# Linear attention by chunks of 128 tokens, its energies and its running state taken by halves of 64

## The chip, the cores and the metric

One Trainium2 chip, one core. The metric is the device time of one execution in microseconds (us): the median of three timed runs of the kernel before is 874.49 us (873.55 to 876.25). The profile shown below is of one further execution.

## The reference, cut to what matters

The layer is an attention block without softmax (B = 16 sequences, N = 512 tokens, D = 128, 16 heads of 8), two layer norms, and a feed-forward part with a shared expert and 8 routed ones (two per token). Only the attention is touched by the change:

```python
q = silu(x @ Wq);  k = silu(x @ Wk);  v = x @ Wv       # 16 heads of 8
q = concat([q * cos(ang), q * sin(ang)])               # 16 features a head, k likewise
energy = einsum('bhnd,bhmd->bhnm', q, k) * tril(ones)
out = einsum('bhnm,bhmd->bhnd', energy, v) @ Wo
out = layernorm(out * sigmoid(x @ G1 @ G2)) * gamma + beta
x = layernorm(x + out)
...
x = layernorm(x + shared_expert(x) + routed_experts(x))
```

There is no softmax, so what all tokens of the past give to a query can be summed up in a state: for each head the 16 x 8 matrix sum of k v. A query takes its own neighbourhood by energies and everything earlier by the state.

## The kernel before, in words

**Stages.** From 0 to about 377 us runs the attention: 64 chunks t of 128 tokens, four to a sequence (c = t mod 4). To about 500 us follow the rest of the routing and of its scatters beside the shared expert, then the routed experts, the rest of the shared expert and the sums at the end. All matrix work is in 32-bit floats, which TensorE does in two passes: a product written once appears twice in the profile.

**The loop** (L791) is software-pipelined. Round t issues, in this order on every engine: `project(t+2)`, one step of the shared expert (`shared`), `turn_over(t+1)`, another step, one step of `after(b)` (output projection, norms, logits of a finished sequence), `energies(t)`, `values(t-1)`, `remember(t+1)`, scatters, more steps of `after` and of the routing. The shared expert feeds from round 14 on: an "up" step is a product of 512 columns with a silu on ACT (L138) or a multiplication on DVE (L150), a "down" step four products of 128 columns (L159). Rounds come in runs of one kind or the other. Engines work their lists in order.

**A chunk.**

- `project`: two products give q, k, the gate and v (L415, L418) into one PSUM tile `pq`; ACT takes out q with a silu (L422), k with a silu (L423), the gate (L426), v into the padded tile `vpad` (L430, 128 partitions) and, one half of the partitions at a time, into `vlow` (L436, twice). DVE multiplies by cosines and sines (L440, tile `hat`). For every second head the k and v rows are turned: the late 64 tokens lie in partitions 0 to 63.
- `turn_over`: four transposes (L453) into `pt`; ACT copies kT (L455), q with one or the other head of each pair set to zero (L459, L460), a copy of a part of that (L461, which waits for L460), and qT (L463).
- `energies`: 16 products (L498) on tiles of 32 rows by 64 columns of the array: four row groups (two heads each) and two halves of the keys, 192 columns each: 64 early queries and 64 late ones of one head, 64 late ones of the other. Each row group g writes a PSUM bank of its own. DVE multiplies each bank with the causal mask (L505, four of 128x384).
- `values`: into `pout`, on tiles of 128 rows by 32 columns (four column groups at once): 4 products of the state with qT, 128 columns (L522, not for c = 0), 8 with `vlow` (L531) and 16 with `vpad` (L540), 64 columns each. ACT copies it out (L546).
- `remember`: 8 products (L476), again 128 by 32, give k v of the whole chunk; DVE masks off the other heads (L483 for c = 0, L486), POOL adds the state so far (L487). For the last chunk of a sequence nothing is done.

**Buffers.** All PSUM tiles but the energies' come from one pool of four banks, `ps_w`: pq, pt, pout, pst and those of the shared expert and of `after`. A new tile takes the bank that was given free first, and its first product waits for that tile's last reader.

Of the kernel before, what the change touches and what calls it, by code (L numbers as in the profile page):

```python
# [10 lines left out]
F32 = mybir.dt.float32  # L11
I32 = mybir.dt.int32
AF = mybir.ActivationFunctionType
# [25 lines left out]
PI_BELOW = 3.141592  # L39

# [6 lines left out]
def tile_kernel(  # L47
# [146 lines left out]
    with ExitStack() as ph:  # L194
# [21 lines left out]
        with tc.manual_schedule(engines=ORDERED):  # L216
# [51 lines left out]

            NVP = 4
            vpads = []  # L270
            for i in range(NVP):
                vp = cst.tile([P, 4, 4, 40], F32, name=f"vpad{i}")

                vl = cst.tile([P, 8, 40], F32, name=f"vlow{i}")
                vpads.append((vp, vl))
                if i < 2:
                    nc.gpsimd.memset(vp, 0.0)
                    nc.gpsimd.memset(vl, 0.0)
# [11 lines left out]
            for vp, vl in vpads[2:]:  # L290
                nought(vp.rearrange("p a b d -> p (a b d)"), 640)
                nought(vl.rearrange("p a d -> p (a d)"), 320)
# [24 lines left out]

        def sines(c):

            for s, (from_, scale, bias) in enumerate([(scratch[:, NC + c], -1.0, half_pi), (scratch[:, c], 1.0, 0.0)]):  # L320
                for to, n0, n1 in ((cst_tok[:, c, 0], 0, D), (cst_tok[:, c, 1, 1::2], D, D + HALF)):
                    nc.scalar.activation(
                        to[:, :, s, :], from_[:, n0:n1].rearrange("p (h d) -> p h d", d=8), AF.Sin,
                        scale=scale, bias=bias,
                    )

        def same(c):

            nc.vector.tensor_copy(
                cst_tok[:, c, 1, 0::2].rearrange("p h s d -> p h (s d)"),  # L330
                cst_tok[:, c, 0, 0::2].rearrange("p h s d -> p h (s d)"),
            )

        with tc.manual_schedule(engines=ORDERED):
            angles(0, pth)
            sines(0)
            angles(1, th_sb)
            same(0)

            causal = cst.tile([P, 3, HALF], F32, name="causal")
            nc.gpsimd.tensor_tensor(causal[:, 0, 0:1], scratch[:, 0, 0:1], zcol, ALU.mult)
            nc.gpsimd.memset(causal, 1.0)
            bmask = cst.tile([P, 64], F32, name="bmask")
            nc.gpsimd.memset(bmask, 1.0)
            nc.gpsimd.affine_select(
                bmask, bmask, pattern=[[-16, 8], [0, 8]], compare_op=ALU.is_ge, fill=0.0, base=0, channel_multiplier=1
            )
            nc.gpsimd.affine_select(  # L350
                bmask, bmask, pattern=[[16, 8], [0, 8]], compare_op=ALU.is_ge, fill=0.0, base=15, channel_multiplier=-1
            )
            for block, at in ((0, 0), (0, HALF), (1, HALF), (2, 0)):
                rows = causal[at : at + HALF, block, :]
                nc.gpsimd.affine_select(
                    rows, rows, pattern=[[1, HALF]], compare_op=ALU.is_ge, fill=0.0, base=0, channel_multiplier=-1
                )
            expi = cst.tile([P, E], I32, name="expi")
            expf = cst.tile([P, E], F32, name="expf")
            first = cst.tile([P, E], F32, name="first")  # L360
            startrow = cst.tile([P, E], F32, name="startrow")
            goes_on = {}
            for n in sorted({(b1 - b0) * NC for b0, b1 in groups}):
                goes_on[n] = cst.tile([P, E, n + 1], F32, name=f"goes_on{n}")
            tri = cst.tile([P, P], F32, name="tri")
            toki = cst.tile([P, NT], I32, name="toki")
            sloti = cst.tile([P, NS], I32, name="sloti")
# [40 lines left out]
        hats, qkt, ets, states, gates, oTs = {}, {}, {}, {}, {}, {}  # L408


        def project(t):
# [11 lines left out]
            nc.scalar.activation(qk[:, D:].rearrange("p (h d) -> p h d", d=16), pq[:, 0:8, 16:32], AF.Silu)  # L423
            if c == 0:
# [4 lines left out]
            vp, vl = vpads[t % NVP]  # L429
            nc.scalar.copy(  # L430
                vp.rearrange("p a (c b) d -> p (a c) b d", b=2)[:, :, :, 0:8],
                pq[:, 8:16, 16:32].rearrange("p h (b d) -> p h b d", b=2),
            )
            for i in range(2):
                mine = slice(HALF * i, HALF * i + HALF)
                nc.scalar.copy(vl[mine, :, 8 * i : 8 * i + 8], pq[mine, 8:16, 16 + 8 * i : 24 + 8 * i])  # L436
# [10 lines left out]
        def turn_over(t):  # L447
# [9 lines left out]
            q2 = wk2.tile([P, 2, 6, HALF], F32, tag="q2", name=f"q2_{t}")  # L457
            halves = pt[:, 0].rearrange("p a (h n) -> p a h n", h=2)
            nc.scalar.activation(q2[:, :, 0:5:4, :], halves, AF.Copy, scale=par[:, 0:1])  # L459
            nc.scalar.activation(q2[:, :, 3:6:2, :], halves, AF.Copy, scale=par[:, 1:2])  # L460
            nc.scalar.copy(q2[:, :, 1:3, :], q2[:, :, 4:6, :])  # L461
# [4 lines left out]
        def remember(t):  # L466

            b, c = divmod(t, NC)
            hat = hats.pop(t)
            if c + 1 == NC:  # L470
                return
            vp = vpads[t % NVP][0]
            pst = ps_w.tile([P, 2, 64], F32, tag="w", name=f"pst_{t}")
            for s in range(2):
                for i in range(4):
                    nc.tensor.matmul(  # L476
                        pst[32 * i : 32 * i + 32, s, :], hat[:, 1, ds(s * P + 32 * i, 32)],
                        vp[:, 2 * s : 2 * s + 2, :, 0:8], start=True, stop=True,
                    )
            states[t] = new = wk3.tile([P, 2, 64], F32, tag="state", name=f"state_{t}")  # L480
            mask = bmask.unsqueeze(1).to_broadcast([P, 2, 64])
            if c == 0:
                nc.vector.tensor_tensor(new, pst, mask, ALU.mult)  # L483
            else:
                add = wk2.tile([P, 2, 64], F32, tag="add", name=f"add_{t}")
                nc.vector.tensor_tensor(add, pst, mask, ALU.mult)  # L486
                nc.gpsimd.tensor_tensor(new, states[t - 1], add, ALU.add)  # L487

        def energies(t):

            kT, q2, _ = qkt[t]
            pes = [ps_e.tile([P, 2, 3, HALF], F32, tag="e", name=f"pe_{t}_{g}") for g in range(4)]
            for s in range(2):
                for g in range(4):
                    rows = slice(32 * g, 32 * g + 32)
                    for i in range(2):
                        mine = slice(HALF * i, HALF * i + HALF)
                        nc.tensor.matmul(  # L498
                            pes[g][mine, s], kT[rows, s, mine], q2[rows, s, 3 * i : 3 * i + 3],
                            start=(s == 0), stop=(s == 1),  # L500
                        )
            ets[t] = []
            for g in range(4):
                et = etp.tile([P, 2, 3, HALF], F32, tag="et", name=f"et_{t}_{g}")
                nc.vector.tensor_tensor(  # L505
                    et.rearrange("p s k n -> p s (k n)"), pes[g].rearrange("p s k n -> p s (k n)"),
                    causal.rearrange("p k n -> p (k n)").unsqueeze(1).to_broadcast([P, 2, 3 * HALF]), ALU.mult,
                )
                ets[t].append(et)

        def values(t):

            b, c = divmod(t, NC)
            et, (vp, vl) = ets.pop(t), vpads[t % NVP]
            vp, vl = vp.rearrange("p a b d -> p (a b d)"), vl.rearrange("p a d -> p (a d)")
            _, _, qT = qkt.pop(t)
            pout = ps_w.tile([P, P], F32, tag="w", name=f"pout_{t}")
            if c > 0:
                state = states.pop(t - 1) if c == NC - 1 else states[t - 1]
                for a in (0, 2, 1, 3):  # L520
                    s = a // 2
                    nc.tensor.matmul(  # L522
                        pout[32 * a : 32 * a + 32, :], state[:, s, ts(a % 2, 32)], qT[:, s, :],
                        start=True, stop=False,
                    )

            for gg in range(2):
                for a in (0, 2, 1, 3):
                    s, g = a // 2, 2 * (a % 2) + gg
                    at = 40 * (4 * s + g) - 16 * gg  # L530
                    nc.tensor.matmul(  # L531
                        pout[32 * a : 32 * a + 32, 0:HALF], vl[:, at : at + 32], et[g][:, s, 0, :],
                        start=(c == 0 and gg == 0), stop=False,
                    )
            for gg in range(2):
                for j in range(2):
                    for a in (0, 2, 1, 3):
                        s, g = a // 2, 2 * (a % 2) + gg
                        at = a * 160 + 32 * (2 * gg + j)
                        nc.tensor.matmul(  # L540
                            pout[32 * a : 32 * a + 32, HALF:], vp[:, at : at + 32], et[g][:, s, 1 + j, :],
                            start=False, stop=(gg == 1 and j == 1),
# [247 lines left out]
        with tc.manual_schedule(engines=ORDERED):  # L790
# [47 lines left out]
            zero = vpads[0][0].rearrange("p a b d -> p (a b d)")[:, 0:N]  # L838
# [271 lines left out]
```

## Time and profile before

| what | value |
|---|---|
| the timed runs, median | 874.49 us (873.55 to 876.25) |
| the profiled execution | 865.53 us, its span 863.8 us |
| granted TensorE clock, mean | 0.988 |
| busy: PE, weight loads, DVE | 825.7, 568.8, 554.2 us |
| busy: ACT, POOL | 433.0, 337.2 us |
| energies, L498 | 2048 passes, 62.6 us busy |
| their masks, L505 | 256 instructions, 124.4 us, 547 ns each |
| values, L522, L531, L540 | 20.4, 26.6, 40.8 us busy |
| chunk's k v, L476 | 768 passes, 20.0 us busy |

Busy time is the time in which an engine had at least one instruction in flight. For PE the passes overlap, so the mean duration of one (340 ns in L498) is far longer than the step from one to the next. "PEld" is the loading of weights, which runs beside the products.

### The profile page before, as it was taken

What the parts mean: (1) busy time and instruction counts of PE and PEld (TensorE: products, weight loads), DVE (VectorE), ACT (ScalarE), POOL (GpSimd) and SP (SyncE); (2) the same over time, 40 slices, a digit from 0 to 9 for tenths busy, and PEclk for the clock granted to TensorE, in tenths of its full rate; (3) what the DMA queues carried; (4) which work ended last, traced back from release to release, by engine and by line L of the source; (5) the groups of instructions that cost most, each with busy time, mean ns of one, the idle gap of its engine ahead of it and who ended that gap; (6) DMA issues with size and microseconds to landing.
All of it is one profiled execution on the core that took longest, in us unless ns stands there. A gap on an engine that the chain in (4) does not pass through costs nothing. (4 is left out here: it accounts for less than half of the span.)

```text
span 863.8 us, 24377 instructions
## 1 busy us (share of the span) xinstructions
PE 825.7 (96%) x9776; PEld 568.8 (66%) x9776; DVE 554.2 (64%) x1629; ACT 433.0 (50%) x1279; POOL 337.2 (39%) x451
## 2 busy tenths in 40 slices
PE   6899999989999998899999998999999999999896
PEld 4666668756766865756666665777667776755664
DVE  7887888889988788975533335444434442387754
ACT  6876776675677677544222222333333333243345
POOL 2132122221666665587666641343333433211110
PEclk9999999999999999999999999999999999999999
DMA  6011111110111110048000032231122200365211
GB/s 199 21 34 33 34 33 33 34 33 15 51 56 56 59 46 21 21 163 295 22 10 6 0 99 79 94 95 53 63 90 93 62 28 25 92 178 169 78 37 49
DMA packets 66387, 57.45 MB, mean 67 GB/s; under 512 B 6180, under 2 KB 55132, under 8 KB 66274
## 3 DMA queue, kind: packets, MB, share of 16 engines
q1 hardware_dynamic: 59474, 44.95, 17.1%
q0 software_dynamic: 6656, 10.69, 3.8%
q8 instruction: 77, 1.26, 0.6%
q10 hardware_dynamic: 144, 0.26, 0.1%
q14 instruction: 36, 0.29, 0.1%
HBM read 32.62 MB, written 26.48 MB: 68 GB/s over the span
## 5 line engine op out<-in xcount | busy, mean ns | idle before, releaser
L725 POOL DMA_INDIRECT xg_dram<-x,idx x128 | 132.3, 1034 | 42.7 <-issue 40.9
L936 POOL DMA_INDIRECT y_dram<-y,to x80 | 77.6, 970 | 155.3 <-ACT y L934 155.3
L138 ACT ACTIVATE sl<-pg 128x512 f32<-128x512 f32 x128 | 75.6, 594 | 121.4 <-PE pg L136 114.7
L150 DVE TENSOR_TENSOR h<-sl,pu 128x512 f32<-128x512 f32 x128 | 87.6, 684 | 74.8 <-PE pu L149 57.7
L136 PE MATMUL pg<-x1T,sg_sb 128*128 128x512 f32 x256 | 132.2, 598 | 0.0
L149 PE MATMUL pu<-x1T,su_sb 128*128 128x512 f32 x256 | 130.9, 593 | 0.0
L159 PE MATMUL pd<-sd_sb,h 128*128 128x128 f32 x1024 | 125.1, 279 | 5.9 <-DVE x1T L164 5.7
L505 DVE TENSOR_TENSOR et<-pe,causal 128x384 f32<-128x384 f32 x256 | 124.4, 547 | 9.1 <-PE pe L498 8.7
L159 PEld LDWEIGHTS pd<-sd_sb,h 128*128 128x128 f32 x1024 | 121.3, 195 | 12.1 <-DVE x1T L164 6.3
L1024 DVE TENSOR_TENSOR eh<-esl,peu 128x512 f32<-128x512 f32 (+1 forms) x96 | 57.5, 599 | 109.8 <-PE peu L1021 107.2
L112 POOL TENSOR_TENSOR rstd<-ve,neghalf 128x4 f32<-128x4 f32 x46 | 49.5, 1076 | 195.1 <-DVE ve L110 188.8
L930 PEld LDWEIGHTS ped<-rd,eh 128*128 128x128 f32 x640 | 84.0, 192 | 24.1 <-issue 22.0
L1019 PE MATMUL peg<-xgT,rg 128*128 128x512 f32 (+1 forms) x192 | 84.6, 522 | 0.0
L1021 PE MATMUL peu<-xgT,ru 128*128 128x512 f32 (+1 forms) x192 | 84.4, 521 | 0.0
L930 PE MATMUL ped<-rd,eh 128*128 128x128 f32 x640 | 84.3, 275 | 0.0
L1023 ACT ACTIVATE esl<-peg 128x512 f32<-128x512 f32 (+1 forms) x96 | 50.5, 526 | 57.5 <-PE peg L1019 54.8
L149 PEld LDWEIGHTS pu<-x1T,su_sb 128*128 128x128 f32 x256 | 45.9, 191 | 44.9 <-issue 39.9
L934 ACT ACTIVATE y<-ped,wt 128x128 f32<-128x128 f32 x80 | 29.4, 367 | 85.7 <-PE ped L930 85.7
L136 PEld LDWEIGHTS pg<-x1T,sg_sb 128*128 128x128 f32 x256 | 44.7, 192 | 37.4 <-issue 34.1
L415 PE MATMUL pq<-W,xT 128*128 128x384 f32 x128 | 59.9, 551 | 7.5 <-DVE h L150 3.2
L498 PE MATMUL pe<-q,kT 32*64 32x192 f32 x2048 | 62.6, 340 | 0.8 <-DVE et L505 0.8
L1021 PEld LDWEIGHTS peu<-xgT,ru 128*128 128x128 f32 x192 | 36.5, 190 | 32.2 <-issue 28.9
(181 smaller groups left out, 1250.8 us busy)
## 6 DMA issues: line engine op xcount, KB each, us to landing
y_dram<-vpad SPq DMA_DIRECT2D x16, 512.0 KB, 7.3
y<-y_dram SPq DMA_DIRECT2D x32, 256.0 KB, 3.3
xT<-xt SPq DMA_DIRECT2D x15, 384.0 KB, 2.9
xg<-xg_dram SPq DMA_DIRECT2D x8, 660.0 KB, 4.5
x<-x SPq DMA_DIRECT2D x16, 256.0 KB, 3.5
o<-res SPq DMA_DIRECT2D x15, 256.0 KB, 2.8
xg_dram<-x,idx POOLq DMA_INDIRECT x128, 2.3
rg<-rg SPq DMA_DIRECT2D x8, 256.0 KB, 4.7
```

The lines of the kernel that those rows point to most:

```text
L136: nc.tensor.matmul(pg, sg_sb[:, ts(i, P)], seq, start=True, stop=True)
L138: nc.scalar.activation(sl, pg, AF.Silu)
L149: nc.tensor.matmul(pu, su_sb[:, ts(i, P)], seq, start=True, stop=True)
L150: nc.vector.tensor_tensor(h[i // half][:, i % half, :], h.pop(("s", i)), pu, ALU.mult)
L159: nc.tensor.matmul(pd, h[k][:, i - k * half, ts(c, P)], sd_sb[:, i, :], start=(i == 0), stop=(i == IS // P - 1))
L498: nc.tensor.matmul(pes[g][mine, s], kT[rows, s, mine], q2[rows, s, 3 * i : 3 * i + 3], start=(s == 0), stop=(s == 1),)
L505: nc.vector.tensor_tensor(et.rearrange("p s k n -> p s (k n)"), pes[g].rearrange("p s k n -> p s (k n)"), causal.rearrange("p k n -> p (k ...
L725: i = nc.gpsimd.indirect_dma_start(out=xg_dram[:, :], out_offset=bass.IndirectOffsetOnAxis(ap=idx[:, k, t : t + 1], axis=0), in_=x1[:, t, ...
L930: nc.tensor.matmul(pd, h[:, i, ts(c, P)], got[e][2][:, i, :], start=(i == 0), stop=(i == IR // P - 1))
L936: i = nc.gpsimd.indirect_dma_start(out=y_dram[:, :], out_offset=bass.IndirectOffsetOnAxis(ap=to[:, at : at + 1], axis=0), in_=y, in_offset ...
L1019: nc.tensor.matmul(pg[:, :n], rg_sb[:, ts(i, P)], xgTs[e][:, ds(o0, n)], start=True, stop=True)
L1021: nc.tensor.matmul(pu[:, :n], ru_sb[:, ts(i, P)], xgTs[e][:, ds(o0, n)], start=True, stop=True)
```

## The change

A chunk stays 128 tokens, but energies are taken only within its halves of 64 tokens; a state is kept at the middle of each chunk as well as at its end, and each half of the queries takes the state just before it. The turned heads are now two neighbours out of each four (they were every second one), so that the two heads of a row group lie alike.

- `project`: k in two silus (64 elements a partition each) to put the heads in the new order; v in four copies of 64 partitions into one tile `vpad` instead of one copy of 128 and two of 64. `vlow` is gone.
- `turn_over`: the copy L461 is gone.
- `energies`: 16 products as before, 128 columns instead of 192; the four banks are by pair of row groups and half, so that two neighbouring row groups write to one bank, each to other partitions. Four masks of 128x256.
- `values`: for each half 4 products with its state (64 columns; none in the first half of a sequence) and 8 with the energies: 24 products for 28, in the first chunk 20 for 24.
- `remember`: two PSUM tiles, one a half, with 16 products of 64 rows by 32 columns of the array (8 of them, one tile, in the last chunk, where there was nothing); two masks (one in the last chunk) and, but for the first half of a sequence, an addition on POOL for each, the second reading the first.
- The masks, the order of the sines and of the columns of Wk, Wv, Wo and theta follow the new order of heads.

```diff
         def project(t):
...
-            nc.scalar.activation(qk[:, D:].rearrange("p (h d) -> p h d", d=16), pq[:, 0:8, 16:32], AF.Silu)
+            for u in range(2):
+                nc.scalar.activation(
+                    qk[:, D:].rearrange("p (a u i d) -> p a u i d", u=2, i=2, d=8)[:, :, u],
+                    pq[:, 0:8, 16 + 8 * u : 24 + 8 * u].rearrange("p (a i) d -> p a i d", i=2), AF.Silu,
+                )
...
-            nc.scalar.copy(
-                vp.rearrange("p a (c b) d -> p (a c) b d", b=2)[:, :, :, 0:8],
-                pq[:, 8:16, 16:32].rearrange("p h (b d) -> p h b d", b=2),
-            )
-            for i in range(2):
-                mine = slice(HALF * i, HALF * i + HALF)
-                nc.scalar.copy(vl[mine, :, 8 * i : 8 * i + 8], pq[mine, 8:16, 16 + 8 * i : 24 + 8 * i])
+            for half in range(2):
+                mine = slice(HALF * half, HALF * half + HALF)
+                for u in range(2):
+                    nc.scalar.copy(vp[mine, :, half ^ u, 8 * u : 8 * u + 8], v[mine, :, u, :])
...
         def turn_over(t):
...
-            nc.scalar.activation(q2[:, :, 0:5:4, :], halves, AF.Copy, scale=par[:, 0:1])
-            nc.scalar.activation(q2[:, :, 3:6:2, :], halves, AF.Copy, scale=par[:, 1:2])
-            nc.scalar.copy(q2[:, :, 1:3, :], q2[:, :, 4:6, :])
+            for i in range(2):
+                nc.scalar.activation(q2[:, :, :, i, :], halves, AF.Copy, scale=par[:, i : i + 1])
...
         def remember(t):
...
-            pst = ps_w.tile([P, 2, 64], F32, tag="w", name=f"pst_{t}")
+            pst = [ps_w.tile([P, 2, 64], F32, tag="w", name=f"pst_{t}_{half}") for half in range(2)]
             for s in range(2):
                 for i in range(4):
-                    nc.tensor.matmul(
-                        pst[32 * i : 32 * i + 32, s, :], hat[:, 1, ds(s * P + 32 * i, 32)],
-                        vp[:, 2 * s : 2 * s + 2, :, 0:8], start=True, stop=True,
-                    )
...
+                    for half in range(2 if c + 1 < NC else 1):
+                        rows = slice(HALF * (half ^ i % 2), HALF * (half ^ i % 2) + HALF)
+                        nc.tensor.matmul(
+                            pst[half][32 * i : 32 * i + 32, s, :], hat[rows, 1, ds(s * P + 32 * i, 32)],
+                            vp[rows, 4 * s : 4 * s + 4, half, 0:16], start=True, stop=True,
+                        )
...
+            state = lasts.get(t - 1) if c > 0 else None
+            for half, kept in enumerate((mids, lasts) if c + 1 < NC else (mids,)):
+                kept[t] = new = wk3.tile([P, 2, 64], F32, tag=f"state{half}", name=f"state_{t}_{half}")
+                add = new if state is None else wk2.tile([P, 2, 64], F32, tag=f"add{half}", name=f"add_{t}_{half}")
+                nc.vector.tensor_tensor(add, pst[half], mask, ALU.mult)
+                if state is not None:
+                    nc.gpsimd.tensor_tensor(new, state, add, ALU.add)
+                state = new
 
         def energies(t):
...
-                    for i in range(2):
-                        mine = slice(HALF * i, HALF * i + HALF)
+                    for k in range(2):
+                        mine = slice(HALF * k, HALF * k + HALF)
+                        half = k ^ g % 2
                         nc.tensor.matmul(
-                            pes[g][mine, s], kT[rows, s, mine], q2[rows, s, 3 * i : 3 * i + 3],
+                            pes[g // 2, half][mine, s], kT[rows, s, mine], q2[rows, s, half],
                             start=(s == 0), stop=(s == 1),
                         )
...
         def values(t):
...
+            for half in range(2):
+                cols = slice(HALF * half, HALF * half + HALF)
+                state = mids.pop(t) if half else lasts.pop(t - 1, None)
+                for g in (0, 2, 1, 3) if state is not None else ():
+                    s, a = divmod(g, 2)
                     nc.tensor.matmul(
+                        pout[32 * g : 32 * g + 32, cols], state[:, s, ts(a, 32)], qT[:, s, cols],
+                        start=(half == 0), stop=False,
                     )
+                for i in range(2):
+                    for g in (0, 2, 1, 3):
+                        s, a = divmod(g, 2)
+                        at = 40 * (2 * (2 * g + i) + half) - 16 * i
                         nc.tensor.matmul(
+                            pout[32 * g : 32 * g + 32, cols], vp[:, at : at + 32], et[a, half][:, s, i, :],
+                            start=(c == 0 and half == 0 and i == 0), stop=(half == 1 and i == 1),
                         )
```

## The prediction, made before the changed kernel ran

> **What bounds the kernel.** I read the slices first. The change touches the chunks' rounds alone, that is the first 44% of the span.
>
> ```profile
> PE   6899999989999998899999998999999999999896
> ...
> DVE  7887888889988788975533335444434442387754
> ```
>
> PE is busy in nearly every slice, but DVE stands at 8 and 9 through the attention, so the question is which of the two is late last. Stretches of that stage say it better: four rounds beside down steps, four beside up steps, then a stretch with routing (columns: us, then busy time of PE, PEld, DVE, ACT, POOL).
>
> ```profile
> 139.00:161.00 22.00, 22.00 (x498) 18.26 (x497) 17.73 (x59) 14.38 (x54) 5.51 (x6) 1.00 0.12 34
> 161.00:184.00 23.00, 23.00 (x463) 14.78 (x461) 19.51 (x61) 17.25 (x61) 5.52 (x6) 1.00 0.11 31
> 184.00:221.00 37.00, 32.85 (x684) 24.76 (x687) 33.94 (x105) 25.02 (x81) 8.97 (x10) 0.95 0.11 31
> ```
>
> PE never rests in the first two; in the third PE rests 4 us, and DVE is the bound. Before round 14 (27 to 83 us), with no shared steps, the timeline shows DVE without a gap for several rounds (42 to 55 us): DVE again. So a PE saving counts beside shared steps, a DVE saving elsewhere.
>
> **The price of a pass.** The timeline of one round, weight loads, shows PE's steps (start, length, group):
>
> ```profile
> 156.34 0.56 PEld L498 LDWEIGHTS pe<-q,kT 32*64 32x64 f32 x32 [0.17 <-issue]
> ...
> 157.18 0.16 PEld L522 LDWEIGHTS pout<-qT,state 128*32 128x32 f32 x8 [0.28 <-issue]
> ...
> 157.32 0.35 PEld L531 LDWEIGHTS pout<-et,vlow 128*32 128x32 f32 x16
> ...
> 157.59 0.52 PEld L540 LDWEIGHTS pout<-et,vpad 128*32 128x32 f32 x32
> ...
> 158.04 0.30 PEld L476 LDWEIGHTS pst<-vpad,hat 128*32 128x32 f32 x16
> ...
> 158.43 0.30 PEld L415 LDWEIGHTS pq<-W,xT 128*128 128x128 f32 x2
> ```
>
> L540's 32 passes take 0.45 us to the next group (158.04 - 157.59): in fours, one to a column group, 0.056 us a four. In narrow windows the same timeline has the state's passes (128 columns) in fours 0.107 to 0.109 us apart, and the energies' (192 columns) in eights 0.163 us apart. So a group costs 0.056, 0.109 or 0.163 us by its columns, and eight run as fast as four where eight tiles are named. A change of tile form costs: after the last eight (begun at 156.89, over at 157.05) L522 begins at 157.18, about 0.09 us of emptying, and its first group is 0.027 us longer than the second; I take 0.115 us. Between L522, L531, L540 and L476, of one form, there is none.
>
> **PE, a chunk.**
> - Energies: 4 groups of 0.163 become 4 of 0.109: -0.216 us, 64 times: -13.8 us.
> - Values: 2 x 0.109 + 12 x 0.056 become 12 x 0.056 (four of them states): -0.218, 48 times; in a sequence's first chunk 12 become 10: -0.112, 16 times. Together -12.3.
> - `remember`: 16 passes in fours become 32. They name eight tiles in a row, as the energies do, so I take eights, again four groups: 0. No row has 64-row tiles; as fours they would cost 0.224 more, 48 times (10.8). The last chunks' 16 passes are new, in fours: 16 x 0.224 = +3.6.
> - Forms: values to `remember` is now a change, 64 times, and `remember` to the logits (L607) 16 times: 80 x 0.115 = +9.2. Ends: 0, if 64 rows need no emptying, and the whole 0.28 of idle loading: +22.4.
>
> Sum -13.3 us; with the ends -22.5 to +10.7.
>
> **DVE.**
>
> ```profile
> L505 DVE TENSOR_TENSOR et<-pe,causal 128x384 f32<-128x384 f32 x256 | 124.4, 547 | 9.1 <-PE pe L498 8.7
> ...
> L486 DVE TENSOR_TENSOR add<-pst,bmask 128x128 f32<-128x128 f32 x32 | 8.9, 278 | 0.0
> ```
>
> These are 128 and 384 columns from PSUM: (547 - 278)/256 = 1.05 ns a column, so 256 take about 412 ns, 135 less, four times: -0.54 us a chunk. One more mask a chunk (0 becomes 1 in the last) holds DVE for 0.20 us (170.63 to 170.83 below; the rest overlaps): -0.34 us a chunk.
>
> **ACT.** L461 (405 ns) goes: qT starts 0.83 us after L460 now (168.62 - 167.78) and would start 0.37 after, as L460 does after L459: -0.46. The second k silu takes between 0.10 (128 columns step 0.157 and 256 step 0.252, carried down to 64) and 0.157. The v copies: the three take 0.60 us, and the two `vlow` ones do not overlap (0.22 each, as against 0.145 for L430). If only a change of partition half prevents it, four take 0.65; if none overlap, 0.92. I take +0.05, end +0.32. The time falls out behind kT, but is added ahead of it: `pq` is freed 0.15 to 0.5 us later.
>
> **POOL** gets four more additions a sequence, 0.46 us each, one chained behind another. They are wanted a round later (5.4 us), and POOL is busy 0.7 at most where it scatters beside the rounds (26.96 of 40 us): hidden. Uncovered they would cost at most 0.46 each, 29 us, but nothing in the queue is that long.
>
> **The new waits.** The two pst tiles turn the ring of four banks differently. In the changed program the transposes of most rounds, and the projection in the round after `po`, take the bank of the first pst tile and so wait for DVE's mask, which stands behind the four energy masks; before, most waited for ACT only. Queued behind that wait are the whole next round of PE, and ACT and DVE behind it. The up-step rounds 28 to 31 show what it meets:
>
> ```profile
> 164.82 0.88 ACT L586 ACTIVATE x<-w,nb,rstd 128x128 f32<-128x128 f32 x2 [0.90 <-DVE nb L582]
> ...
> 166.70 1.03 PEld L555 LDWEIGHTS po<-wo_sb,oT 128*128 128x128 f32 x8 [0.50 <-ACT vlow L436]
> ...
> 168.76 1.95 DVE L505 TENSOR_TENSOR et<-pe,causal 128x384 f32<-128x384 f32 x4 [0.78 <-PE pe L498]
> ...
> 170.10 0.30 PEld L415 LDWEIGHTS pq<-W,xT 128*128 128x128 f32 x2
> ...
> 170.63 0.28 DVE L486 TENSOR_TENSOR add<-pst,bmask 128x128 f32<-128x128 f32 x1
> 170.83 0.67 DVE L559 SCALAR_TENSOR_TENSOR o<-gate,po 128x512 f32<-128x512 f32 x1
> ```
>
> I moved these rows by the sums above. The four masks take about 1.41 instead of 1.95 us, the first state mask ends 1.61 us after their start.
> - Round 28: PE would gain 0.32, but `po` (L555) waits for the v copies, behind x's norms on ACT, behind DVE's nb. That chain is only 0.34 us earlier on DVE and pays about 0.15 on ACT: gain 0.20.
> - Round 29: masks from 168.35, the state's ends at 169.96, and the projection, ready at 169.68, goes at 170.0 instead of 170.10. Gain left 0.10.
> - Round 30: PE pays the last chunk's `remember` and two changes of form; the next transposes wait for the mask at 176.88, 0.12 us later than before.
> - Round 31: DVE, without a gap since 173.4, frees the bank at 182.2; the transposes go at 182.25 against 182.23.
>
> So of 0.83 us saved by PE in four rounds nothing is left beside up steps. With the ACT ends the same walk gives +0.42 us, without the waits -0.83.
>
> Beside down steps (139 to 161 us) DVE has 4.3 us to spare: the walk gives -0.63 for four rounds. Without shared steps DVE gives its 0.34 four times, less some of the new waits: -1.0. In the rounds with routing (198 to 219 and 335 to 363 us, some six) DVE's 0.34 each.
>
> **Sum.** Rounds 2 to 13: 3 x -1.0 = -3.0. Down-step rounds: 4 x -0.63 = -2.5. Routing: -2.0. Up-step rounds, about 28: 7 x 0 (-5.8 to +2.9). Together -7.5 us, 16 x 4 chunks. What follows (377 to 864 us) is untouched and PE works through, so it only moves forward. Startup loses two ACT clearings and four POOL ones, under 1 us beside the loads: nothing. From the profiled 865.53 us that is 858.0; the timed median stands 1% above the profiled run, and the share carried over, 874.49 x 858.0 / 865.53, gives **867 us**.
>
> **The skill against it.** The banks are the one place where a rule speaks against the change. In this trace four column groups write to one bank at full step (L540), but each row group has a bank of its own (L498). The Trainium skill (TensorEngine Tiling (Array Packing), section Restrictions and Gotchas, Gotcha 1) says that different row tiles cannot access the same PSUM bank simultaneously. Here neighbouring row groups share banks, on other partitions; no run shows that yet. By the rule the energies go in fours and the kernel is the slower one of the rivals; by the row of L540, where partitions keep the writers apart, it is not.
>
> **Rivals.**
> 1. *The whole PE sum arrives.* The waits are met, since DVE falls by 22 us in all (64 x 0.34) and could run ahead. -13.3: 861 us; with half the changes of form free, 856. Against it: DVE's bursts behind `after` (L104, L567, L572) stay where they are. Chance 0.18.
> 2. *The gain is eaten.* ACT's copies overlap nowhere and up-step rounds lose 0.42: 2.9 us back; if also the early rounds gain only half, -7.5 + 2.9 + 1.5 = -3, and with waits 0.2 us longer in 28 rounds +2.5. So 871 to 877, in the middle 874. Chance 0.28: 0.18 within 0.3%, 0.10 slower.
> 3. *Slower: two row groups on one bank do not run together.* Energies take 8 groups of 0.109, 0.437 us more than I forecast, 64 times 28.0; `remember` 10.8 more; -13.3 + 38.8 = +25.5: 900 us. It decides from the point where energies take more than 0.65 us a chunk, what they take now. For it: before, no two row groups shared a bank. Against: the writers are on different partitions. Chance 0.12.
> 4. The forecast, 863 to 871: 0.42.
>
> **Chances and range.** Faster by over 0.3% (about what the measurement can tell from no change): 0.42 + 0.18 = 0.60; within it 0.18; slower 0.10 + 0.12 = 0.22. The range takes in rivals 1 and 2 and leaves out the third: 856 to 879.
>
> **What would show it.** Energies: 32 passes in eights 0.11 us apart, L522's successor 0.62 us after their start, not 0.84; at 0.22 apart the third rival is true. `remember`: 32 passes within 0.25 us. The masks at 412 ns. PE waits in the projection and the transposes put down to DVE's state masks, 0.2 to 0.4 us in two rounds of four beside up steps; if they are missing, rival 1. `po` still waiting on the v copies. Wrong altogether if the time lies in what follows 377 us.

## The result and the profile after

The changed kernel takes **874.31 us** (20 runs, 872.90 to 877.52), the kernel before on the same chip 874.14 us (20 runs, 872.60 to 877.22): ratio 1.000, 95% interval 0.999 to 1.001. No gain was measured where 0.86% was forecast.

Two rows of the profile after (span 871.4 us), the slices:

```profile
PE   6889999999999999999999998999999999999896
...
DVE  7688887789777778865533325444444442387654
```

PE is still busy nearly everywhere; DVE has become lighter through the attention. One round without scatters, weight loads, in the timeline of the changed kernel (start us, length, engine, line, operation, count, idle time before):

```profile
158.50 0.45 PEld L505 LDWEIGHTS pe<-q,kT 32*64 32x64 f32 x32 [0.76 <-issue]
159.12 0.16 PEld L530 LDWEIGHTS pout<-qT,state 128*32 128x32 f32 x8 [0.17 <-issue]
159.20 0.30 PEld L538 LDWEIGHTS pout<-et,vpad 128*32 128x32 f32 x16
159.43 0.18 PEld L530 LDWEIGHTS pout<-qT,state 128*32 128x32 f32 x8
159.54 0.30 PEld L538 LDWEIGHTS pout<-et,vpad 128*32 128x32 f32 x16
159.93 0.29 PEld L479 LDWEIGHTS pst<-vpad,hat 64*32 64x32 f32 x32
160.31 0.30 PEld L418 LDWEIGHTS pq<-W,xT 128*128 128x128 f32 x2
```

From one start to the next: energies 0.62 us (0.84 before), values with their new change of form 0.81 (0.86), `remember` 0.38 with twice the passes (0.39). The two groups whose count or length the change moves:

```profile
L513 DVE TENSOR_TENSOR et<-pe,causal 128x256 f32<-128x256 f32 x256 | 90.5, 416 | 13.3 <-PE pe L505 13.0
...
L490 POOL TENSOR_TENSOR state<-state,add 128x128 f32<-128x128 f32 x96 | 44.1, 459 | 137.9 <-DVE add L488 133.9 <-ACT lg L609 1.2
```

Masks fell from 547 to 416 ns, POOL's additions rose from 32 to 96. So each piece is there, and up to round 33 the starts of the energies run ahead of the profile before: 3.8 us there. From round 39 it is lost: 1.7 us behind at round 50, 4.0 at round 63. Rounds 40 to 43 take 24.10 us after and 22.39 before. Those are rounds in which POOL scatters rows (L723, two a round). Round 44 of the changed kernel shows what happens (here and below, rows in between are left out):

```profile
258.02 0.97 POOL L723 DMA_INDIRECT xg_dram<-x,idx  x1 [0.31 <-issue]
258.18 0.45 PEld L505 LDWEIGHTS pe<-q,kT 32*64 32x64 f32 x32 [0.76 <-issue]
258.80 0.16 PEld L530 LDWEIGHTS pout<-qT,state 128*32 128x32 f32 x8 [0.17 <-issue]
258.88 0.17 PEld L538 LDWEIGHTS pout<-et,vpad 128*32 128x32 f32 x2
259.53 0.25 PEld L538 LDWEIGHTS pout<-et,vpad 128*32 128x32 f32 x12 [0.48 <-issue]
259.67 0.76 DVE L513 TENSOR_TENSOR et<-pe,causal 128x256 f32<-128x256 f32 x2 [0.63 <-PE pe L505]
```

The energies are handed to PE at the usual pace (L530 is 0.62 us behind L505), but DVE, idle for 0.63 us, gets them only 1.49 us after their first load instead of 0.74, and PE itself stops taking passes in the middle of the values, for 0.48 us, waiting for nothing that the profile names. PE goes on 0.54 us after the scatter's row has ended at 258.99, DVE 0.14 us behind it. A row of the timeline shows when a pass was handed over; when it is done is seen by who was waiting for it. Below, **the lateness** of a kernel is summed over rounds 38 to 63: how much later than in rounds without scatters the first energies are reported done (usual: 0.71 us behind the first load in the changed kernel, 0.89 in the kernel before; only delays over 0.1 us count). It is 17.7 us in this profile. In the profile of before it is 0.7 us, all of it in round 57, where no scatter is in flight and the loads themselves stop in between.

### The profile page after: what moved, and what is told of

The parts are those of the page before. It is cut to its first block, busy times and chain, and to the rows that moved or that the text cites. A ratio compares the mean times of both kernels' runs of the same rounds, so it can differ in the third digit from the quotient of the medians.

```text
span 871.4 us, 25785 instructions
## 1 busy us (share of the span) xinstructions
PE 825.9 (95%) x10288; PEld 563.5 (65%) x10288; DVE 538.8 (62%) x1693; ACT 414.6 (48%) x1341; POOL 361.6 (41%) x511
## 5 line engine op out<-in xcount | busy, mean ns | idle before, releaser
L723 POOL DMA_INDIRECT xg_dram<-x,idx x128 | 129.1, 1009 | 39.9 <-issue 38.2
L490 POOL TENSOR_TENSOR state<-state,add 128x128 f32<-128x128 f32 x96 | 44.1, 459 | 137.9 <-DVE add L488 133.9
L513 DVE TENSOR_TENSOR et<-pe,causal 128x256 f32<-128x256 f32 x256 | 90.5, 416 | 13.3 <-PE pe L505 13.0
L418 PE MATMUL pq<-W,xT 128*128 128x384 f32 x128 | 60.8, 558 | 4.0 <-ACT qT L467 2.0
L538 PE MATMUL pout<-et,vpad 128*32 128x64 f32 x2048 | 55.7, 222 | 6.3 <-issue 6.1
```

The source lines that it names most:

```text
L418: nc.tensor.matmul(pq[:, :, 0:24], xts[b][:, c, 0:P], W[:, 0:384].rearrange("p (h n) -> p h n", n=24), start=True, stop=True)
L513: nc.vector.tensor_tensor(et.rearrange("p s i n -> p (s i) n"), pes[a, half].rearrange("p s i n -> p (s i) n"), causal.unsqueeze(1).to_bro ...
L723: i = nc.gpsimd.indirect_dma_start(out=xg_dram[:, :], out_offset=bass.IndirectOffsetOnAxis(ap=idx[:, k, t : t + 1], axis=0), in_=x1[:, t, ...
```

## The experiments

Theory A: two row groups on one PSUM bank are held up under scatters. Theory B: POOL's additions, queued with the scatters, hold PE up. Theory C: the gain goes into the waits on DVE's state masks. Theory D came later. Each set of runs had one chip and its own runs of the kernel before; no two of the sets below share a chip. Moving energies to other banks mixes heads, so those kernels compute other numbers; they serve for times alone.

### First set: banks, adder, no scatters (before: 866.8 us)

Own banks, in `energies` of the changed kernel:

```diff
-                            pes[g // 2, half][mine, s], kT[rows, s, mine], q2[rows, s, half],
+                            pes[g // 2, g % 2][mine, s], kT[rows, s, mine], q2[rows, s, half],
```

> The changed kernel with one edit: each row group of the energies writes to a PSUM bank of its own again, as before the change. Sizes, counts, masks and order are the same; the energies of two heads in four then meet the values of other heads, so the numbers that come out are others. Theory A: in the rounds with scatters the energies are held up because two row groups share a bank; in the changed kernel their completion (first weight load to the semaphore that DVE waits for) goes from 0.71 us to between 0.87 and 2.23 us there. By A all rounds show 0.71 us here, values take 0.6 us and not up to 2, and the kernel comes to 867 to 870 us. Theory B: POOL's additional state additions, queued with the scatters, hold PE up: nothing changes, 874 us, and the delays stay. Theory C: the gain goes into the waits on DVE's state masks: nothing changes either.

862.2 us, ratio 0.9955 (0.9942 to 0.9969). Energies done after 0.68 us in nearly all rounds, never later than 0.83. This looked like theory A, but the changed kernel itself had not run on this chip.

Shared banks in the kernel before:

```diff
-                            pes[g][mine, s], kT[rows, s, mine], q2[rows, s, 3 * i : 3 * i + 3],
+                            pes[g ^ i][mine, s], kT[rows, s, mine], q2[rows, s, 3 * i : 3 * i + 3],
```

> The kernel before with one edit: the second key half of each row group's energies goes to the neighbouring row group's bank, so that two row groups write to each bank, to other partitions; nothing else moves (energies and values of neighbouring heads are mixed up by it, so the numbers are others). Theory A: in the 25 rounds with scatters the energies, never late before, end 0.2 to 1.5 us late, about 0.6 us in the mean less what slack takes: 5 to 15 us more, 880 to 890 us. Theories B and C: no change, 874 us.

868.1 us, ratio 1.0011 (0.9996 to 1.0027), lateness 0.7 us, all in round 57 as in the kernel before. It seemed to speak against theory A; the next set showed that it decides nothing.

State additions on DVE (`nc.vector` for `nc.gpsimd` in L490):

> The changed kernel with its state additions on DVE instead of POOL. Theory A: the energies stay late in the rounds with scatters; POOL's scatters start 0.5 to 0.9 us earlier, so the delays change size and move, and DVE pays 96 additions of some 0.2 us, partly in its slack: 870 to 880 us. Theory B: the pauses in values vanish: 866 to 870 us. Theory C: DVE is later with its masks and the time grows by 2 to 5 us.

876.0 us, ratio 1.0108 (1.0086 to 1.0130). The energies are on time (lateness 0.6 us), yet it is slower: the 96 additions now take time of DVE (rounds 20 to 23 take 22.66 us, with POOL adding 22.16).

No scatters in the rounds (the two calls of `scatter_behind` after `remember` taken out):

> The changed kernel with the two scatters taken out of every round; all of them run after the attention, so the total grows by up to 60 us and only the rounds are read. Theory A, and any theory in which the scatters are what holds PE up: the energies end 0.71 us after their first load in every round, and rounds 40 to 43 take some 1.7 us less than with scatters, 22.1 to 22.4 us. If the delays stay, the scatters only mark the place and the cause is another.

One run, 913.3 us with the scatters at the end. All energies after 0.71 us, rounds 40 to 43 in 22.06 us. Right, but the next set showed that on such a chip scatters cost next to nothing anyway (22.10 us in those rounds).

### Second set: the changed kernel itself on another chip (before: 869.0 us)

> The changed kernel itself once more, beside the others on one chip. Ratio to the kernel before 1.000, as measured first (0.999 to 1.001); the energies late in the same rounds, by the same amounts (round 43: 1.78 us instead of 0.71). If they are late in other rounds, or not at all, the delay belongs to the one profile and not to the kernel.

862.5 us, **ratio 0.9928** (0.9906 to 0.9950): the same program is faster here. Its lateness is 0.6 us. Round 52, with a scatter that starts 0.29 us after the first load of the energies:

```profile
302.03 0.45 PEld L505 LDWEIGHTS pe<-q,kT 32*64 32x64 f32 x32 [0.76 <-issue]
302.32 0.97 POOL L723 DMA_INDIRECT xg_dram<-x,idx  x1 [0.30 <-issue]
302.65 0.16 PEld L530 LDWEIGHTS pout<-qT,state 128*32 128x32 f32 x8 [0.17 <-issue]
302.74 0.30 PEld L538 LDWEIGHTS pout<-et,vpad 128*32 128x32 f32 x16
302.81 1.41 DVE L513 TENSOR_TENSOR et<-pe,causal 128x256 f32<-128x256 f32 x4
```

DVE has the energies 0.78 us after the first load, before the scatter's row is over (303.29). So the hold is not in the program alone. It also means that own banks had cured nothing in the first set, and that shared banks could do no harm there: on such a chip there was nothing to see. Theory C falls here: PE's waits for the state masks are longer than in the first measurement (8.7 us for the transposes and projections, 7.0 there), and the gain is there all the same.

Two more on this chip. 192 columns in the energies again (`q2[rows, s]` from block `half` to `half + 3`, masks on two of the three blocks):

> The changed kernel with 192 columns a product in the energies again (64 of them twice, the masks leave them out), two row groups on one bank as in the changed kernel; the numbers are the reference's. The kernel before with shared banks (192 columns) showed no delay under scatters, the changed kernel (128 columns) did. If the width decides, the energies end at one and the same time, about 0.93 us after their first load, in all rounds. If sharing decides whatever the width, they are up to 1.5 us late in the rounds with scatters, as in the changed kernel. Rounds without scatters cost 0.2 us more by either.

One run: 870.2 us; energies done after 0.93 us everywhere. As to the hold it tells nothing, this chip showing none. As to the price it tells much: rounds 28 to 31 take 22.92 us, in the changed kernel 22.06: 0.86, four times 0.215.

Other pairs of row groups on a bank (`pes[g % 2, k ^ g // 2]`):

> The changed kernel with other pairs of row groups on a bank: 0 with 2 and 1 with 3 instead of 0 with 1 and 2 with 3, each to other partitions (energies of other heads meet the values, so the numbers are others). If any two row groups on one bank are held up under scatters, the delays stay, up to 1.5 us. If only neighbours are, the energies end 0.7 us after their first load in every round.

One run: 862.2 us, energies after 0.75 us, at most 0.16 later under scatters. No pair is held up, but then nothing is on this chip.

Scatters ahead of the additions on POOL:

```diff
+                if left:
+                    scatter_behind(oTs[(t - 1) // NC][:, ds((t - 1) % NC * P, 1)])
+                    scatter_behind()
                 if 0 <= t + 1 < NT:
                     remember(t + 1)
-                if left:
-                    scatter_behind(oTs[(t - 1) // NC][:, ds((t - 1) % NC * P, 1)])
-                    scatter_behind()
```

> The changed kernel with a round's two scatters ahead of its state additions on POOL instead of behind them. Theory A (energies that share banks are held until a scatter in flight is over): the scatters start about 0.5 to 0.9 us earlier in a round and end before the next energies complete, the delays of 0.2 to 1.5 us are gone, and the time is that of the kernel with own banks, a ratio of 0.995 to the kernel before. The additions wait for the scatters, but are wanted only in the next values, some 1.5 us later. Theory B (additions behind scatters hold PE up): slower than the changed kernel by 0.5 us a round with scatters, a ratio of 1.01.

863.6 us, ratio 0.9948 (0.9927 to 0.9969): as fast as the changed kernel within the intervals. Theory B expected it slower by 0.5 us a round with scatters, which did not come; but this chip holds nothing up, so the proof is left to the fourth set.

### Third set: a chip like the first one (before: 873.9 us)

> The kernel before itself, for a profile from the chip on which the two others of this set run. If the kernel before takes 873 to 876 us here, as in the first measurement, this profile says where it is slower than in the profile shown (865.5 us): by the theory that scatters hold PE up in both kernels on such a chip, in rounds 38 to 63, by 8 us. If it takes 865 to 870 us, as beside the other experiments, the profile is that of before again within 1 us at round 63 and 3 us at the end.

> The changed kernel itself. If the kernel before takes 865 to 870 us on this chip, the changed one takes 0.5 to 0.9% less, 860 to 864 us, and its energies are at most 0.2 us late under scatters. If the kernel before takes 873 to 876 us here, the ratio is 1.000 again and the energies are up to 1.5 us late.

> The kernel of own banks once more, now beside the changed kernel on one chip. If sharing a bank costs nothing but where scatters hold PE up, it takes the same as the changed kernel within 0.1% where that one is 0.7% faster than before; where that one is no faster (a chip as in the first measurement), own banks are 0.4 to 1% faster than it. If sharing costs by itself, 0.03 us a round as the completions show (0.68 against 0.71 us): 2 us less, 0.2%, on any chip.

The kernel before took 873.7 us under the profile, its lateness is 8.2 us: some 0.7 us in every fourth round from 38 to 54, 0.1 in round 48, and 0.3 to 1.35 us in most rounds from 57 on (round 57 is as late in the profile of before). In round 42 its values stop in the middle, as in the changed kernel:

```profile
249.15 0.98 POOL L725 DMA_INDIRECT xg_dram<-x,idx  x1 [0.30 <-issue]
249.65 0.16 PEld L522 LDWEIGHTS pout<-qT,state 128*32 128x32 f32 x8 [0.28 <-ACT q L460]
249.79 0.33 PEld L531 LDWEIGHTS pout<-et,vlow 128*32 128x32 f32 x10
...
250.40 0.21 PEld L531 LDWEIGHTS pout<-et,vlow 128*32 128x32 f32 x6 [0.28 <-issue]
```

In the profile of before shown first, the same 16 passes of that round went through in one piece:

```profile
249.00 0.35 PEld L531 LDWEIGHTS pout<-et,vlow 128*32 128x32 f32 x16
```

The changed kernel: 872.8 us, ratio 0.9982 (0.9967 to 0.9997), lateness 16.4 us. Own banks: 873.0 us, ratio 0.9988 (0.9972 to 1.0005), lateness 16.2 us. **Theory A falls**: with a bank for each row group the energies are held just as long. What is left is **theory D**: on some chips no energies are reported done from the start of a scatter until about 0.55 us after its row (in the late rounds of the changed kernel 0.4 to 0.7 us mostly, in those of the kernel before some 0.3 to 0.5); the changed kernel's scatters stand in the way in nearly every round, those of the kernel before mostly in every fourth.

### Fourth set: where the scatters stand in the round (before: 874.2 us)

> The changed kernel itself beside them. 0.993 of before where before takes 865 to 870 us, 0.998 to 1.000 where before takes 873 to 876 us.

872.4 us, ratio 0.9984 (0.9972 to 0.9995), lateness 16.7 us.

The kernel before, its scatters made later:

```diff
+                    for _ in range(2 if scatters else 0):
+                        nc.gpsimd.tensor_tensor(junk, ident, ident, ALU.add)
                     scatter_behind(oTs[(t - 1) // NC][:, ds((t - 1) % NC * P, 1)])
```

> The kernel before with two additional POOL additions of 128x128 (0.46 us each, read by nobody) ahead of a round's scatters, which so start about 0.9 us later, where the changed kernel's start. Theory D: where the kernel before takes 873 to 876 us its energies are then late in most of the 25 rounds with scatters instead of every fourth, by 0.5 to 1 us: 6 to 15 us more, a ratio of 1.007 to 1.017. Where it takes 865 to 870 us: 1.000. If the changed kernel's form is what scatters hold up, 1.000 on both.

879.0 us, ratio 1.0052 (1.0037 to 1.0068), lateness 11.2 us. Right in sign, smaller than expected: two rounds of four are late, not most. The lateness grew by 3.0 us and the time by 4.8, so this run alone doesn't part the later scatters from the two additions. But an unchanged form of the energies is held in other rounds now, and more of them, once the scatters come later.

The changed kernel with scatters ahead of the additions ("e13" in texts below):

> The kernel with the scatters ahead of the state additions, again. On a chip where the kernel before takes 873 to 876 us theory D expects late energies only in every fourth round (round 43: 1.2 us instead of 0.71) and a ratio of about 0.993; on the other chips 0.995 as measured. By any theory in which the scatters' place does not matter it is that of the changed kernel.

**863.7 us, ratio 0.9884** (0.9869 to 0.9899), lateness 2.8 us: better than the 0.993 expected. Round 44 of it:

```profile
252.19 0.99 POOL L723 DMA_INDIRECT xg_dram<-x,idx  x1 [0.53 <-issue]
253.48 0.97 POOL L723 DMA_INDIRECT xg_dram<-x,idx  x1 [0.30 <-issue]
254.46 0.92 POOL L490 TENSOR_TENSOR state<-state,add 128x128 f32<-128x128 f32 x1
254.56 0.45 PEld L505 LDWEIGHTS pe<-q,kT 32*64 32x64 f32 x32 [0.76 <-issue]
255.18 0.16 PEld L530 LDWEIGHTS pout<-qT,state 128*32 128x32 f32 x8 [0.17 <-issue]
255.26 0.30 PEld L538 LDWEIGHTS pout<-et,vpad 128*32 128x32 f32 x16
255.59 1.41 DVE L513 TENSOR_TENSOR et<-pe,causal 128x256 f32<-128x256 f32 x4
```

The second scatter ends at 254.45, just ahead of the energies; its 0.55 us are over before they are done, and the values run through. The addition L490 on POOL runs beside all of these energies, which are done 0.71 us after their first load as usual: **theory B falls**. Against 872.4 us for the changed kernel on the same chip, with the same instructions, the order alone is worth 8.7 us here.

The scatters moved further ahead, behind the first energy mask:

```diff
                     energies(t)
+                    scatter_behind(ets[t][0, 0][:, 0, 0, 0:1])
+                    scatter_behind()
...
-                    scatter_behind(oTs[(t - 1) // NC][:, ds((t - 1) % NC * P, 1)])
-                    scatter_behind()
```

> The changed kernel with a round's two scatters moved ahead of the values: they start when the first energy mask of the round is done, and the state additions stand behind them on POOL. Theory D (on some chips PE finishes no energies from the start of a scatter until about 0.55 us after its end): the pair then runs from about 1.2 to 3.6 us after the first load of the energies, 4.2 us with the 0.55, and the next energies come at 5.5 us, so none are late on any chip; 0.9 to 1.0% faster than before where the kernel before takes 873 to 876 us, and as fast as the changed kernel, 0.7% under before, where it takes 865 to 870 us. If the time is lost to something else on such chips, the ratio stays at 0.998 to 1.000 there.

866.1 us, ratio 0.9910 (0.9896 to 0.9925), lateness 3.3 us. The time is the expected one, but not the freedom from lateness: nine rounds are late. The first mask starts up to 3 us behind the energies where DVE is busy, and POOL waits for it (1.43 us ahead of round 44), so the second scatter of that pair ends at 256.08 us, 0.37 us into the energies of round 44 (first load 255.71), where e13's ends 0.10 us before them.

### Last two sets: the order alone (before: 868.9 and 874.0 us)

The same move of the two calls in the kernel before:

> The kernel before with its two scatters of a round ahead of the state addition on POOL, as e13 does it with the changed kernel. Theory D: its scatters start 0.5 us earlier; where the kernel before takes 873 to 876 us, late in every fourth round by about 0.7 us, some 3 of its 8 us come back: a ratio of 0.995 to 0.998. Where it takes 865 to 870 us: 1.000. If it came to 0.99 there, e13's gain would be the order's alone and the halves of 64 would have no share in it.

> The changed kernel with its scatters first, beside it: 0.988 of before where the kernel before takes 873 to 876 us, 0.995 where it takes 865 to 870 us. The halves' own share is the difference of the two: 0.8% by theory D on both kinds of chip.

868.4 us, ratio 1.0005 (0.9987 to 1.0023), and for the changed kernel 863.2 us, 0.9954 (0.9935 to 0.9973). On a chip of the other kind:

> The kernel before with its scatters first, again, for a chip of the other kind. Theory D: where the kernel before takes 873 to 876 us, 0.995 to 0.998 of it; where it takes 865 to 870 us, 1.000 as measured. If it comes to 0.99 on a chip of the first kind, the gain of the changed kernel with scatters first is there mostly the order's.

869.8 us, ratio 0.9948 (0.9930 to 0.9967), lateness 3.6 us. So there the order alone is worth 0.5%, and the halves of 64 another 0.6% (0.9884 / 0.9948 = 0.9936, the two ratios from two chips of this kind), about what they are worth on the other chips; the 0.8% expected of them is not reached.

All together; times in us by how long the kernel before takes on the chip, lateness in brackets:

| kernel | chips with 867 to 869 | chips with 874 |
|---|---|---|
| before | 866.8, 869.0, 868.9 (0.7 in the profile of before) | 874.1, 873.9, 874.2, 874.0 (8.2 in the profile of the third set) |
| changed | 862.5 (0.6) | 874.3, 872.8, 872.4 (17.7, 16.4, 16.7) |
| before, scatters first | 868.4 (0.0) | 869.8 (3.6) |
| changed, scatters first | 863.6, 863.2 (0.6, 0.5) | 863.7 (2.8) |
| before, scatters later | | 879.0 (11.2) |

The changed kernel with its scatters first is the one that is faster than before on both kinds, by 0.5% and 1.2%; on the first kind it doesn't differ from the changed kernel beyond the intervals.

## Why the prediction was wrong

Most prices of single pieces held. What failed is what the additions on POOL push, and where the time of the profiled run and of the timed runs parted. The measured 874.31 us lies in the band of the second rival, but not by its mechanism: ACT's copies do overlap, and where nothing is held the gain is there.

- **Energies**: 0.62 us a chunk as forecast; the third rival (row groups on one bank in turn) is false. The Trainium skill (TensorEngine Tiling (Array Packing), section Restrictions and Gotchas, Gotcha 1) has different row tiles never in one bank at a time; here they wrote to one bank, on other partitions, at full step: done after 0.71 us, with own banks after 0.68, and 872.8 against 873.0 us in all. The saving lands where PE bounds: giving it back cost 0.86 us in four rounds.
- **Values, `remember`**: 0.05 us a chunk less where 0.10 was forecast (0.218 less 0.115 for the form); 32 passes in eights at no more time, as forecast.
- **DVE and ACT**: masks 416 ns (412 forecast); four v copies in 0.65 us, two k silus in 0.33, as taken.
- **The waits on state masks** came, with 4.4 us for the transposes and 2.6 for the projections over the whole run. Four rounds beside up steps gain 0.34 (forecast 0), beside down steps 0.33 (0.63), rounds 32 to 37 in most profiles 0.9 (2.0), in the others nothing. Up to round 14 the profiles of the changed form stand between 0.2 us behind the profile of before and 2.0 ahead instead of 3.0 ahead, the loss at the start (next point) counted in; left out are the two that give DVE or PE more work. The reading "DVE again" for 42 to 55 us was thin: PE is busy there for all of the 13.00 us, DVE for 12.90. Nor did 184 to 221 us show DVE as the bound: it is idle for 3.1 us there itself.
- **Startup**, put at nothing, costs 1.4 us by the medians: in all profiles of the changed form the energies of round 2 begin at 27.3 to 29.1 us, in those of before at 26.0 to 26.8. The ring of banks again: at the start the third projection now takes the bank of a transpose and waits for `qT` on ACT (read in one profile of the changed form: L418 at 24.57 us, against L415 at 23.82 before). I had walked that ring through rounds 28 to 31 alone.
- **POOL, the step that failed first**: "hidden", since the additions are wanted a round later and POOL has room. True of the additions. But they stand ahead of the scatters, and push them on into the next energies: 16.4 to 17.7 us of lateness on 874 chips, 2.8 with the scatters first. That a scatter can hold PE up was in no step: the profile of before, with no round late under a scatter, could not show it.
- **The share carried over, the step that failed with it**: "the timed median stands 1% above the profiled run, and the share carried over". By its time and its lateness the profile is one of a chip with 868 us; the three timed runs are of a chip with 874. The 8.2 us between the profile of before and that of the third set are not spread over the kernel: 4.5 us have come up by the start of round 63 (371.5 and 376.1 us), nearly all of them in rounds with scatters, 1.6 more with the next scatters up to 385 us; the last 2 come mostly at the start of the routed experts, where profiles from 868 chips differ among themselves by nearly as much (1.7 us between that of before and that with shared banks). The 1% that was carried over as a share was the sign that something costs time which the profile doesn't show, and a change that moves it had to be priced by it. On the chip where the changed kernel itself ran with 869 us before, the forecast holds: 0.87% by the profile's own time, 0.72% measured (0.50 to 0.94). In part this is luck: the early rounds, the start, the down steps and the routing brought less than their terms, the up steps more.
- **The sum on 874 chips** comes out of the two: the changed form saves what it saves elsewhere, some 6 us, and its lateness is 8 to 9.5 us above that of before (16.4 to 17.7 less 8.2), part of it in slack: 0 to 1.8 us of gain remain.
- **After 377 us** nothing changes: from the start of round 63 to the end all profiles of both kernels take 492 to 497 us, but for the run that leaves its scatters for then.

Still open: why some chips hold PE up and others don't, and whether it is the chip at all: no chip is on record with two occasions, so something that comes and goes with time would look the same. Scatters' rows are as long on both (0.97 to 1.04 us mostly), and their first packet starts 0.57 to 0.62 us after the row on both. The Trainium skill (Perfetto Trace Analysis, section Per-engine timelines) says that such a row ends with the last descriptor written and not with the data moved, and the packets' start agrees. PE goes on at about the moment at which the first packets start; what ties the two together no run here shows.

## What to carry to other kernels

Before carrying a share from a profile to timed runs, make sure that both come from conditions under which the kernel takes the same time; where they part, find the stage that parts them first. An instruction added to an engine with room costs nothing by itself, but what is queued behind it moves: look at what that then meets, and put the work that disturbs others first and the work that can wait last. A change to a ring of buffers is walked through every stage, the start too, not only through the steady rounds.

## What the runs showed of the hardware

- On four chips of seven (counting the first measurement as one) the energies' products of 32 rows by 64 columns weren't reported done until about 0.55 us after a scatter's row: in the changed kernel up to 1.5 us late. On the other three they are at most 0.16 us late under scatters. Rows of 1.4 to 1.5 us instead of 0.97 occur on both kinds.
- Two row groups that write to one bank, on other partitions, cost 0.03 us a round and no more (0.71 against 0.68 us).
- 64 rows by 32 columns of the array run in eights: 32 passes loaded in 0.29 us, as long as 16 passes in fours.
- Products of the whole array are reported late too, only that nothing is lost by it there. Between 396 and 497 us some 57 scatters run beside the shared expert's products, and PE's loads in the third set's profile of before stay 6.15 us behind those of the profile shown first all along (here 440.28 and 446.43 us). But DVE, which waits for the sums, gets them six times 0.45 to 0.94 us later than that. One of them, first in the profile shown first, then in the other:

```profile
440.28 1.98 PEld L159 LDWEIGHTS pd<-sd_sb,h 128*128 128x128 f32 x17
441.48 0.29 DVE L164 TENSOR_TENSOR x1T<-pd,x 128x128 f32<-128x128 f32 x1 [1.50 <-PE pd L159]
```

```profile
446.43 1.98 PEld L159 LDWEIGHTS pd<-sd_sb,h 128*128 128x128 f32 x17
446.65 0.99 POOL L725 DMA_INDIRECT xg_dram<-x,idx  x1 [0.16 <-issue]
448.11 0.29 DVE L164 TENSOR_TENSOR x1T<-pd,x 128x128 f32<-128x128 f32 x1 [1.97 <-PE pd L159]
```

The loads are 6.15 us apart, DVE's starts 6.63. So the hold isn't one of the energies' small tiles alone; whether the products or only the reports of them come late, and on which of them PE stops, no run here shows.
